# A four-layer conv and attention network on one core: attention's preparation and settling in smaller parts, and the second layer's gate laid between the first norms of the feed-forward layer

## The chip, the cores and the metric

The kernel runs on one core of a Trainium2 chip. The time is the device time of one execution in microseconds (us), the median of several runs. PE is TensorE (matmul), PEld its weight load, DVE is VectorE, ACT is ScalarE, POOL is GpSimd, SP is SyncE, which here issues DMAs. All data is float32.

## The reference, cut to what matters

X has 4 images of 128 channels and 64 x 64 places; as tokens these are 4 x 4096 rows of 128. Four layers follow each other. The change touches the end of the second, the start of the third and the attention of the fourth.

```python
# layer 1, its end: o is the scan's output, normed over the batch
g = sigmoid(einsum('bihw,io->bohw', o, conv4_w) + conv4_b)
x = g * x + x
# layer 2, per token: t is the normed token
a = t + cumprod(cos(t + theta))        # heads of 8, the first replaced by the last
x1 = layernorm(a);  q = cos(phi) * cos(x1[:8])
t = t + layernorm(x1 + relu(q @ w1.T + b1) @ w2.T + b2)
# layer 3, attention over 4096 tokens of one image
f = v @ W1[:h];  g = v @ W1[h:]        # 16 numbers per token, v the normed token
e[i, j] = exp(sum_a w2[a] * tanh(f[i, a] + g[j, a] + b1[a]) + b2)   for j < i
t[i] += sum_j e[i, j] * v[j] / (sum_j e[i, j] + 1e-10)
```

## The kernel before

X stays in SBUF, [128, 4 x 4096]. `layer1`, `layer2` and `attention` issue most of their work through `InOrder` (L69 on), which keeps every engine's queue in the order of the source. In the profile all of these instructions therefore stand under line L82, and are told apart by the names of their tiles.

**The gate, end of `layer1` (L1419 to L1444).** The scan leaves its output in DRAM, 32 blocks of 512 columns, `kept` (L1314 stores `o`). After the batch statistics (`mv`, `sc`, `sb`, L1404 to L1416) `gate(k)` loads one block (`oin`, L1422, four buffers), multiplies by `conv4_w` into `psg`, takes the sigmoid on ACT (`g`) and computes X = (g + 1) X on DVE. `to_tokens(k - 2)` turns the block before the last into tokens with four transposes (`psf`), copied back into X by DVE for odd and by ACT for even blocks. 34 steps, each with a gate and a turn, but for the two ends.

**The feed-forward layer, `layer2`.** X is now 128 tiles of 128 tokens; a group is 8 tiles (two of the gate's blocks). `slot(p, s)` (L1730) is written out by hand: p is the group, s one of eight slots. Slot s does the matmuls and rectifiers of group p, and steps of the groups around it: the first norm of group p + 3 (`moments A` in slot 0, `variance`, `root` in slot 3, `a_norm` in 4, `a_turns`, `a_less`), the cosines and products of group p + 2 (slot 0: Abs and Sin on ACT, `a_products` on POOL), its second norm (B, slots 2 to 5), and the third (D) of group p - 1. The loop starts at p = -3, so three passes come before the first matmul (`phh`, `hid`, `pff`). Its weights w1T and w2T are loaded by SP at the start (L118, L1539).

**Attention, `attention` (L1994).** For each image there are 8 query blocks of 512 tokens (`ib`, called block 0 to 7). Block ib runs over the keys in 4 ib + 3 rounds (`blocks`, L2124): 4 ib + 1 of full width, one with the parts 384 and 128 wide, one 256 wide. 544 rounds in all. The tanh is split into factors, so that a round (`products`, L2133) is: 4 row groups of matmuls of the maps F and G give the denominators in D (three banks) and the numerators `num` of the round two before; ACT takes Ln of D and Exp of the result (r, 128 x 1536, together with the finished e of an earlier round 128 x 2048); DVE multiplies r by num (128 x 1024 and 128 x 512); POOL adds the three parts. Two rounds later ACT's Exp gives e, DVE masks the diagonal (`keep`, four masks, in rounds 1 to 3 of the next block), and PE multiplies e by v (`acc`).

`side` chooses which of the two sets of banks of D a round uses; they share two banks. The fourth bank is also the one in which everything else is turned or mapped (`aux`). A round in which it is so used (`taken`), and the one behind it, stay on side 0. Where a round uses the same side as the last (`again`), its order on PE differs, since it must wait for the last Ln.

Two kinds of work are laid between the rounds. `prepare(n, q)` (L2089) makes the next block's v, F and G: for even q `statistics` (L2071, 8 bn_stats, 6 small DVE operations, Ln and Exp for rstd), v from X (4 operations, part 1), transposes and vT (part 2), four maps (parts 3 to 6: matmul, Exp on ACT, then the largest value into `top` on DVE, and for G a product on POOL), an end (7). `settle` (L2233) turns the weighted sum: `zs`, `den`, `zl`, and the additions into X, seven rounds after a block's last. These lines spread the parts:

```python
PARTS, ON_BANK = 8, (2, 3, 4, 5, 6)
to = -(-PARTS * max(r - first + 1, 0) // (rounds - first))
step((n, ib, parts, r == rounds - 1), range(done, max(done, to)))
```

Of the kernel before, what the change touches and what calls it, by code (L numbers as in the profile page):

```python
# [8 lines left out]
F32 = mybir.dt.float32  # L9
# [7 lines left out]
P = 128  # L17
NB = 4
# [70 lines left out]
class Kernel:  # L89
# [816 lines left out]

    def layer1(self):

# [4 lines left out]
        nc = plain  # L917
        NG = 8
        GS = NT // NG
        with ExitStack() as ctx:  # L920
            cp = ctx.enter_context(tc.tile_pool(name="l1c", bufs=1))
            sp = ctx.enter_context(tc.tile_pool(name="l1s", bufs=2))
            gp = ctx.enter_context(tc.tile_pool(name="l1g", bufs=2))
            kp = ctx.enter_context(tc.tile_pool(name="l1k", bufs=2))
            dram = ctx.enter_context(tc.tile_pool(name="l1d", bufs=1, space=DRAM))
            pm = ctx.enter_context(tc.tile_pool(name="l1pm", bufs=4, space=PSUM))
            pp = ctx.enter_context(tc.tile_pool(name="l1pp", bufs=1, space=PSUM))

# [2 lines left out]

            lin1_w = self.load(cp, "lin1_w", [P, P])
            fc_in4 = self.load(cp, "fc_in4", [P, P])
            conv4_w = self.load(cp, "conv4_w", [P, P])


            wx = self.load(cp, "in_w4", [P, 2, 257])
# [466 lines left out]
            mv = sp.tile([P, 2], F32, name="mv")  # L1404
            nc.vector.bn_aggr(mv, bst)
            sc = sp.tile([P, 1], F32, name="sc")
            sb = sp.tile([P, 1], F32, name="sb")
            nc.scalar.activation(sc, mv[:, 1:2], AF.Sqrt, bias=self.eps5)
            nc.vector.reciprocal(sc, sc)
            nc.vector.tensor_mul(sc, sc, self.col("bn_g"))  # L1410
# [3 lines left out]
            nc.tensor.matmul(ps[:, 0:1], conv4_w, sb, start=True, stop=True)  # L1414
            nc.vector.tensor_add(sb, ps[:, 0:1], self.col("conv4_b"))
            nc.vector.tensor_scalar(conv4_w, conv4_w, sc, None, ALU.mult)  # L1416
            nc = InOrder(tc)

            def gate(k):  # L1419
                ks = slice(k * 512, (k + 1) * 512)  # L1420
                o = gp.tile([P, 512], F32, name="oin", tag="tm", bufs=4)
                plain.sync.dma_start(o, kept[k])  # L1422
                ps = mm("psg")
                nc.tensor.matmul(ps, conv4_w, o, start=True, stop=True)
                g = gp.tile([P, 512], F32, name="g", tag="yT")
                nc.scalar.activation(g, ps, AF.Sigmoid, bias=sb)
                nc.vector.scalar_tensor_tensor(X[:, ks], g, 1.0, X[:, ks], ALU.add, ALU.mult)

            def to_tokens(k):
                ps = mm("psf")  # L1430
                for v in range(4):
                    c = k * 512 + v * P
                    nc.tensor.transpose(ps[:, v * P:(v + 1) * P], X[:, c:c + P], self.ident)
                dst = X[:, k * 512:(k + 1) * 512]
                if k % 2:
                    nc.vector.tensor_copy(dst, ps)
                else:
                    nc.scalar.copy(dst, ps)

            for k in range(NB * NG + 2):  # L1440
                if k < NB * NG:
                    gate(k)
                if k >= 2:
                    to_tokens(k - 2)  # L1444

    def flip(self):

# [65 lines left out]
    def layer2(self):  # L1513
# [8 lines left out]
        with ExitStack() as ctx:  # L1522
# [22 lines left out]
            cphi = cp.tile([P, 8], F32, name="cphi")  # L1545
            self.cos(cp, cphi, self.row("phi"), [P, 8], "cphi")

            nc = InOrder(tc)
            V, S, G = nc.vector, nc.scalar, nc.gpsimd

            def bcast(name):
# [1 line left out]

            def stream(g):
                return T[:, g * GT:(g + 1) * GT, :]

            st = {}

# [165 lines left out]
            def on(g, step, *args):  # L1724
                if 0 <= g < NG:
                    step(*([g] + list(args)))

            ON_VECTOR = ((0, 1, 3), (1,), (1,), (1, 3), (1,), (1,), (1, 3), (1,))

            def slot(p, s):  # L1730
# [47 lines left out]
                else:  # L1778
                    on(a, a_less)
                    on(b, b_turns)  # L1780

            for p in range(-3, NG + 1):
                for s in range(8):
                    slot(p, s)

# [206 lines left out]
    def attention(self):  # L1994
# [14 lines left out]
        with ExitStack() as outer:  # L2009
# [7 lines left out]
            with ExitStack() as ctx:  # L2017
# [52 lines left out]

                def statistics(t0):  # L2071

                    st = sp.tile([P, 8, 6], F32, name="st")
                    mean = sp.tile([P, 8], F32, name="mean")
                    rstd = sp.tile([P, 8], F32, name="rstd")
                    d = sp.tile([P, 8], F32, name="d")
                    for k in range(8):
                        nc.vector.bn_stats(st[:, k, :], T[:, t0 + k, :])
                    nc.vector.tensor_add(mean, st[:, :, 1], st[:, :, 4])
                    nc.vector.tensor_scalar(mean, mean, 0.5, None, ALU.mult)  # L2080
                    nc.vector.tensor_sub(d, st[:, :, 1], st[:, :, 4])
                    nc.vector.tensor_mul(d, d, d)
                    nc.vector.tensor_add(rstd, st[:, :, 2], st[:, :, 5])
                    nc.vector.scalar_tensor_tensor(rstd, d, 32.0, rstd, ALU.mult, ALU.add)
                    nc.scalar.activation(rstd, rstd, AF.Ln, bias=self.eps5, scale=1.0 / P)
                    nc.scalar.activation(rstd, rstd, AF.Exp, scale=-0.5)
                    norm[0] = mean, rstd

                def prepare(n, q):  # L2089

                    v = vs[q]
                    if q % 2 == 0:
                        statistics(n * NT + 4 * q)
                    yield
                    mean, rstd = norm[0]
                    for k in range(4):
                        t = n * NT + 4 * q + k
                        nc.vector.tensor_scalar(v[:, k, 0:LAST], T[:, t, 0:LAST], mean[:, t % 8:t % 8 + 1],
                                                rstd[:, t % 8:t % 8 + 1], ALU.subtract, ALU.mult)
                    yield  # L2100
                    pd = aux()
                    for k in range(4):
                        aside(nc.tensor.transpose(pd[:, k * P:(k + 1) * P], v[:, k, :], self.ident))
                    vT = rp.tile([P, 512], F32, name="vT", bufs=1)
                    uses[:] = [nc.vector.tensor_copy(vT, pd)]
                    wrote[0] = None
                    yield
                    out = {"v": v, "F": [], "G": []}
                    for k, (to, m) in enumerate((("F", wf[0]), ("F", wf[1]), ("G", wg[0]), ("G", wg[1]))):
                        ps = aux()  # L2110
                        aside(nc.tensor.matmul(ps, m, vT, start=True, stop=True))
                        t = bp.tile([P, 512], F32, name=f"{to}{k % 2}" + (f"_{q}" if to == "G" else ""),
                                    bufs=1 if to == "G" else 3)
                        uses[:] = [nc.scalar.activation(t, ps, AF.Exp, scale=2.0)]
                        wrote[0] = t
                        out[to].append(t)
                        yield
                        nc.vector.tensor_reduce(top[:, 8 * n + q, k:k + 1], t, AX.X, ALU.max)
                        if to == "G":
                            nc.gpsimd.tensor_scalar(t, t, cw[k % 2], None, ALU.mult)  # L2120
                    pieces[n, q] = out
                    yield
# [110 lines left out]
                def settle(n, ib, aT):  # L2233
# [4 lines left out]
                    zs = ep.tile([P, 512], F32, name="zs", bufs=1)  # L2238
                    uses[:] = [nc.vector.tensor_copy(zs, z)]
                    wrote[0] = None  # L2240
                    z = zs.rearrange("p (s c) -> p s c", c=P)
                    den = sm.tile([P, 4], F32, name="den")
                    nc.vector.tensor_scalar(den, z[:, :, LAST], tiny, None, ALU.add)
                    nc.vector.reciprocal(den, den)
                    zl = sm.tile([P, 4], F32, name="zl")
                    nc.vector.tensor_reduce(zl, z[:, :, 0:LAST], AX.X, ALU.add)
                    nc.vector.tensor_mul(zl, zl, den)
                    t0 = n * NT + 4 * ib
                    for s in range(4):
                        tt = T[:, t0 + s, 0:LAST]  # L2250
# [5 lines left out]


                order = [(n, q) for n in range(NB) for q in range(8)]
                for _ in prepare(*order[0]):
                    pass  # L2260
                later = [lambda *a: a, weigh, settle]
                LAG = 4 + len(later)
                waiting, sums = [None, None], [None, None]
                spaces = [rp.tile([P, 4, 512], F32, name="r", bufs=RB) for k in range(2)]
                held = [None] * len(later)
                PARTS, ON_BANK = 8, (2, 3, 4, 5, 6)
                last = [0, False]

                def step(block, parts=()):


                    taken = held[-1] is not None or any(p in ON_BANK for p in parts)
                    side = int(last[0] == 0 and not taken and not last[1])
                    again = side == last[0]
                    last[:] = side, taken
# [6 lines left out]
                        next(ahead)  # L2282

                for k, (n, ib) in enumerate(order):
                    ahead, done = (prepare(*order[k + 1]), 0) if k + 1 < len(order) else (None, PARTS)
                    todo = list(blocks(ib))
                    rounds = len(todo)

                    first = 4 + LAG if ib == 7 else 0
                    for r, parts in enumerate(todo):  # L2290
                        to = -(-PARTS * max(r - first + 1, 0) // (rounds - first))
                        step((n, ib, parts, r == rounds - 1), range(done, max(done, to)))
                        done = max(done, to)
                for k in range(LAG):
                    step(None)
                nc = self.nc
# [110 lines left out]
@with_exitstack  # L2407
def tile_conv_attn_hybrid(ctx: ExitStack, tc: tile.TileContext, ins: dict, out: bass.AP):
    k = Kernel(ctx, tc, ins, out)
    k.layer0()  # L2410
    k.layer1()
    k.layer2()
    k.attention_maps(ctx)
    k.moe(2)
    k.attention()
    k.moe(3)
    k.flip()
# [79 lines left out]
```

## Time and profile before

| | us |
|---|---|
| median of 3 runs (lowest, highest) | 5567.05 (5563.71, 5577.1) |
| the profiled execution: its time, its span | 5584.88, 5583.2 |
| layer 1's scan and what is before it, to the end of the statistics | 0 to 1937.8 |
| the gate | 1937.8 to 1985.8 |
| three passes of norms before the steady feed-forward layer | 1985.8 to 2050.5 |
| feed-forward layer in its steady state, last pff at | 2691 |
| attention, first and last multiplication by num | 3093.1 to 5192.5 |
| the second expert layer's last pex, the flip to the output | 5542, to 5583.2 |

PE is busy 4990.0 us (89% of the span), DVE 4020.2, ACT 3113.5, POOL 3102.9; the mean granted TensorE clock is 0.941. A row of a timeline gives start, duration, engine, source line, operation, written and read tiles, their shape and a count, and in brackets how long the engine had been idle before it and what released it. A row of the stages gives the stretch, its length and the busy time of PE, PEld, DVE, ACT and POOL, each with its number of instructions, then the clock granted to PE (1 is full), the DMA share and GB/s. A row of waits gives who waited for whom, the total in us, how often, and the longest.

### The profile page before, as it was taken

Reading aid. Unit: us, or ns where it says so; the run is one execution under the profiler, and the core shown is the slowest. Engines: PE = TensorE matmul, PEld = TensorE weight load, DVE = VectorE, ACT = ScalarE, POOL = GpSimd, SP = SyncE. Lnnn points to the kernel's source line nnn. Section 1 sums busy time; section 2 is a strip of 40 time slices with the busy share of each in tenths; the row PEclk is TensorE's granted clock in tenths of the full one; section 3 lists DMA queues with packets and bytes.
Section 4 is the critical chain, followed back from the end, with each engine's and each line's share of the span. In section 5 each row is a group of like instructions: output and inputs, shape, how many; then the busy total and the mean of one; then the engine's idle time right before and its main releaser. Section 6 shows DMA issues by size and latency. Waiting matters only on the chain. (4 is left out here: it accounts for less than half of the span.)

```text
span 5583.2 us, 62833 instructions
## 1 busy us (share of the span) xinstructions
PE 4990.0 (89%) x21718; PEld 2405.5 (43%) x21718; DVE 4020.2 (72%) x7854; ACT 3113.5 (56%) x3785; POOL 3102.9 (56%) x3027
## 2 busy tenths in 40 slices
PE   5898999879999859999887899989998998999887
PEld 3454444436666523333443344434443444444443
DVE  6888898758875577886697665666566666665796
ACT  1221222146654445555421789878988997889431
POOL 0625355414443334543498567666766776667597
PEclk8999999989988779999899899999999999999899
DMA  5545455300000110000000000000000000000001
GB/s 173 133 124 127 127 143 129 83 6 5 12 16 16 41 44 1 1 1 1 6 31 31 1 1 1 1 1 1 1 1 1 1 1 1 1 1 1 5 1 61
DMA packets 66743, 185.21 MB, mean 33 GB/s; under 512 B 13158, under 2 KB 16038, under 8 KB 64744
## 3 DMA queue, kind: packets, MB, share of 16 engines
q1 hardware_dynamic: 55792, 163.68, 9.9%
q0 software_dynamic: 6272, 12.86, 1.4%
q10 hardware_dynamic: 4344, 4.50, 0.3%
q8 instruction: 175, 2.87, 0.2%
q14 instruction: 160, 1.31, 0.1%
HBM read 131.63 MB, written 49.36 MB: 32 GB/s over the span
## 5 line engine op out<-in xcount | busy, mean ns | idle before, releaser
L82 POOL TENSOR_TENSOR r<-r 128x512 f32<-128x512 f32 (+1 forms) x1088 | 1348.7, 1241 | 666.1 <-DVE r L82 610.3
L82 DVE TENSOR_TENSOR r<-r,num 128x1024 f32<-128x1024 f32 (+1 forms) x1088 | 969.9, 926 | 565.0 <-PE num L82 518.1
L82 PE MATMUL D<-F,G 32*128 32x512 f32 (+3 forms) x4608 | 1223.1, 591 | 1.9 <-POOL G L82 1.0
L82 PE MATMUL num<-F,G 32*128 32x512 f32 (+3 forms) x4608 | 1090.1, 606 | 105.0 <-DVE r L82 101.0
L82 ACT ACTIVATE r<-r 128x2048 f32<-128x2048 f32 (+4 forms) x610 | 1018.4, 1679 | 49.2 <-POOL r L82 3.4
L82 ACT ACTIVATE r<-D 128x1536 f32<-128x1536 f32 (+1 forms) x544 | 764.2, 1405 | 210.4 <-PE D L82 178.2
L82 PE MATMUL acc<-pr,ident 128*128 128x512 f32 x1600 | 736.2, 609 | 63.2 <-DVE pr L82 63.0
L82 PEld LDWEIGHTS D<-F,G 32*128 32x128 f32 x4608 | 505.3, 190 | 326.0 <-issue 216.3
L82 PE MATMUL acc<-r,v 128*128 128x512 f32 (+3 forms) x1152 | 608.1, 615 | 2.9 <-DVE aT L82 2.9
L82 PEld LDWEIGHTS num<-F,G 32*128 32x128 f32 x4608 | 394.8, 187 | 414.0 <-DVE r L82 236.1
L1887 PE MATMUL pex<-w_expert_w,vT 128*128 128x512 f32 x1024 | 490.8, 619 | 77.6 <-DVE x L1890 77.5
L1897 POOL TENSOR_TENSOR x<-x 128x512 f32<-128x512 f32 (+2 forms) x576 | 472.3, 820 | 103.5 <-DVE x L1890 73.4
L82 POOL DMA_INDIRECT px<-tab,idx x196 | 359.4, 1834 | 295.1 <-DVE idx L82 158.5
L82 PEld LDWEIGHTS acc<-pr,ident 128*128 128x128 f32 x1600 | 303.7, 195 | 414.1 <-issue 330.3
L82 DVE TENSOR_TENSOR pr<-v,wt 128x2560 f32<-128x2560 f32 x160 | 453.9, 2843 | 30.7 <-PE acc L82 23.6
L82 PE MATMUL pff<-hid,w_ffn_w2T 128*128 128x512 f32 x1024 | 468.9, 601 | 0.0
L1890 DVE TENSOR_TENSOR x<-pex,gate 128x1024 f32<-128x1024 f32 x256 | 309.0, 1213 | 61.5 <-POOL X L1898 49.9
L82 PEld LDWEIGHTS acc<-r,v 128*128 128x128 f32 x1152 | 177.6, 191 | 395.8 <-issue 266.3
L1887 PEld LDWEIGHTS pex<-w_expert_w,vT 128*128 128x128 f32 x1024 | 184.8, 194 | 328.0 <-DVE x L1890 174.2
L82 ACT ACTIVATE hid<-phh,cols 128x512 f32<-128x512 f32 x320 | 198.9, 685 | 224.7 <-PE phh L82 224.7
L82 POOL TENSOR_TENSOR Y<-y,tm 128x64 f32<-128x64 f32 x256 | 115.4, 471 | 331.9 <-DVE w L82 159.9
L82 POOL TENSOR_TENSOR X<-X,sl 128x512 f32<-128x512 f32 x32 | 90.1, 2817 | 376.1 <-ACT sl L82 376.1
(563 smaller groups left out, 7390.4 us busy)
## 6 DMA issues: line engine op xcount, KB each, us to landing
v<-tab SPq DMA_DIRECT2D x320, 256.0 KB, 3.9
oms<-omw SPq DMA_DIRECT2D x32, 432.0 KB, 3.3
omr<-oms SPq DMA_DIRECT2D x32, 432.0 KB, 4.4
X<-in_x_dram SPq DMA_DIRECT2D x8, 1024.0 KB, 10.6
tab<-vb SPq DMA_DIRECT2D x64, 128.0 KB, 2.7
o<-o SPq DMA_DIRECT2D x32, 256.0 KB, 2.0
oin<-o SPq DMA_DIRECT2D x32, 256.0 KB, 2.8
kept<-X SPq DMA_DIRECT2D x4, 2048.0 KB, 6.3
```

What stands on the lines that cost most here:

```text
L82: return lambda *args, **kwargs: self.tc.keep_in_program_order(op(*args, **kwargs))
L1887: nc.tensor.matmul(pex[:, 4 * h:4 * h + 4, :], vT[:, k, :], ew[:, 512 * h:512 * (h + 1)], start=True, stop=True)
L1890: nc.vector.tensor_tensor(x, pex, gate[:, k, :].unsqueeze(2).to_broadcast([P, NE, P]), ALU.mult)
L1897: nc.gpsimd.tensor_tensor(x[:, 0:w, :], x[:, 0:w, :], x[:, w:2 * w, :], ALU.add)
```

## The change

The gate leaves `layer1`, which only keeps `conv4_w`, `sb` and the DRAM blocks alive (`gate_maps`). `layer2` runs four gate steps before its first pass, and then 11, 11 and 8 between the slots of the three passes. All turned blocks are now copied by ACT. `psg` and `psf` use the four banks of `phh`. The statistics of attention are cut in three parts (numbered -3 to -1, even q only), the empty first part of odd q is gone, settling is cut in three steps over three rounds (`settle`, `ratio`, `onto`), and the parts are dealt out one a round from the first round on, as soon as they fit, instead of evenly over the block.

```diff
-            nc = InOrder(tc)
-            def gate(k):
...
-            def to_tokens(k):
...
-            for k in range(NB * NG + 2):
-                if k < NB * NG:
-                    gate(k)
-                if k >= 2:
-                    to_tokens(k - 2)
+            self.gate_maps = conv4_w, sb, kept
...
+            def gate(k):
+                if k < NK_:
+                    ks = slice(k * 512, (k + 1) * 512)
+                    o = gp.tile([P, 512], F32, name="oin", bufs=4)
+                    plain.sync.dma_start(o, kept[k])
+                    ps = ph.tile([P, 512], F32, name="psg", tag="phh")
+                    nc.tensor.matmul(ps, conv4_w, o, start=True, stop=True)
+                    x = gp.tile([P, 512], F32, name="g")
+                    S.activation(x, ps, AF.Sigmoid, bias=gate_b)
+                    V.scalar_tensor_tensor(self.X[:, ks], x, 1.0, self.X[:, ks], ALU.add, ALU.mult)
+                if k >= 2:
+                    ps = ph.tile([P, 512], F32, name="psf", tag="phh")
+                    for v in range(4):
+                        c = (k - 2) * 512 + v * P
+                        nc.tensor.transpose(ps[:, v * P:(v + 1) * P], self.X[:, c:c + P], self.ident)
+                    S.copy(self.X[:, (k - 2) * 512:(k - 1) * 512], ps)
...
+            GATES, LAST_GATES = (0, 1, 1, 1, 2, 2, 2, 2), (0, 1, 1, 1, 2, 2, 1, 0)
...
+            steps = iter(range(NK_ + 2))
+            for _ in range(4):
+                gate(next(steps))
             for p in range(-3, NG + 1):
                 for s in range(8):
                     slot(p, s)
+                    for _ in range(GATES[s] if p < -1 else LAST_GATES[s] if p < 0 else 0):
+                        gate(next(steps))
...
                 def statistics(t0):
                     st = sp.tile([P, 8, 6], F32, name="st")
+                    for h in range(2):
+                        for k in range(4 * h, 4 * h + 4):
+                            nc.vector.bn_stats(st[:, k, :], T[:, t0 + k, :])
+                        yield
...
-                    for k in range(8):
-                        nc.vector.bn_stats(st[:, k, :], T[:, t0 + k, :])
...
                     norm[0] = mean, rstd
+                    yield
...
                     if q % 2 == 0:
-                        statistics(n * NT + 4 * q)
-                    yield
+                        yield from statistics(n * NT + 4 * q)
...
                     wrote[0] = None
-                    z = zs.rearrange("p (s c) -> p s c", c=P)
+                    return n, ib, zs.rearrange("p (s c) -> p s c", c=P)
+
+                def ratio(n, ib, z):
                     den = sm.tile([P, 4], F32, name="den")
...
                     nc.vector.tensor_mul(zl, zl, den)
+                    return n, ib, z, den, zl
+
+                def onto(n, ib, z, den, zl):
...
-                later = [lambda *a: a, weigh, settle]
+                later = [lambda *a: a, weigh, settle, ratio, onto]
...
-                PARTS, ON_BANK = 8, (2, 3, 4, 5, 6)
+                PARTS = 7
...
-                    taken = held[-1] is not None or any(p in ON_BANK for p in parts)
+                    taken = held[SETTLES] is not None or any(1 <= p <= 5 for p in parts)
...
-                        to = -(-PARTS * max(r - first + 1, 0) // (rounds - first))
-                        step((n, ib, parts, r == rounds - 1), range(done, max(done, to)))
-                        done = max(done, to)
+                        now = ()
+                        if ahead is not None and r >= first:
+                            now = range(done, done - (done - PARTS) // (rounds - r))
+                            done = now.stop
+                        step((n, ib, parts, r == rounds - 1), now)
```

`done` starts at 0 for odd q and at -3 for even q of the block that is prepared, and at round `first` = 13 (11 before) in block 7.

More of the change, by code (lines that the diff above doesn't have):

```diff
@@ L905, in layer0_gather, with layer1 @@
                         nc.vector.tensor_add(xs, xs, sl)
-    def layer1(self):
+    def layer1(self, after):
         tc, X = self.tc, self.X
@@ L919, in layer1 @@
         GS = NT // NG
+        dram = after.enter_context(tc.tile_pool(name="l1d", bufs=1, space=DRAM))
+        ga = after.enter_context(tc.tile_pool(name="l1a", bufs=1))
         with ExitStack() as ctx:
@@ L924, in layer1 @@
             kp = ctx.enter_context(tc.tile_pool(name="l1k", bufs=2))
-            dram = ctx.enter_context(tc.tile_pool(name="l1d", bufs=1, space=DRAM))
             pm = ctx.enter_context(tc.tile_pool(name="l1pm", bufs=4, space=PSUM))
@@ L933, in layer1 @@
             fc_in4 = self.load(cp, "fc_in4", [P, P])
-            conv4_w = self.load(cp, "conv4_w", [P, P])
+            conv4_w = self.load(ga, "conv4_w", [P, P])
             wx = self.load(cp, "in_w4", [P, 2, 257])
@@ L1406, in layer1 @@
             sc = sp.tile([P, 1], F32, name="sc")
-            sb = sp.tile([P, 1], F32, name="sb")
+            sb = ga.tile([P, 1], F32, name="sb")
             nc.scalar.activation(sc, mv[:, 1:2], AF.Sqrt, bias=self.eps5)
@@ L1416, in layer1 @@
             nc.vector.tensor_scalar(conv4_w, conv4_w, sc, None, ALU.mult)
-            nc = InOrder(tc)
-            def gate(k):
[L1420 to L1427, printed above, removed]
-            def to_tokens(k):
[L1430 to L1438, printed above, removed]
-            for k in range(NB * NG + 2):
-                if k < NB * NG:
-                    gate(k)
-                if k >= 2:
-                    to_tokens(k - 2)
+            self.gate_maps = conv4_w, sb, kept
     def flip(self):
@@ L1546, in layer2 @@
             self.cos(cp, cphi, self.row("phi"), [P, 8], "cphi")
-            nc = InOrder(tc)
+            plain, nc = nc, InOrder(tc)
             V, S, G = nc.vector, nc.scalar, nc.gpsimd
@@ L1555, in stream @@
                 return T[:, g * GT:(g + 1) * GT, :]
+            conv4_w, gate_b, kept = self.gate_maps
+            gp = ctx.enter_context(tc.tile_pool(name="l2g", bufs=2))
+            NK_ = len(kept)
+            def gate(k):
[14 more added lines that the diff above has]
+                    S.copy(self.X[:, (k - 2) * 512:(k - 1) * 512], ps)
             st = {}
@@ L2258, in attention @@
                 order = [(n, q) for n in range(NB) for q in range(8)]
+                PARTS = 7
                 for _ in prepare(*order[0]):
                     pass
-                later = [lambda *a: a, weigh, settle]
+                later = [lambda *a: a, weigh, settle, ratio, onto]
+                SETTLES = 2
                 LAG = 4 + len(later)
@@ L2284, in attention @@
                 for k, (n, ib) in enumerate(order):
-                    ahead, done = (prepare(*order[k + 1]), 0) if k + 1 < len(order) else (None, PARTS)
+                    ahead = done = None
+                    if k + 1 < len(order):
+                        ahead, done = prepare(*order[k + 1]), 0 if order[k + 1][1] % 2 else -3
                     todo = list(blocks(ib))
@@ L2410, in tile_conv_attn_hybrid @@
     k.layer0()
-    k.layer1()
-    k.layer2()
+    with ExitStack() as gate:
+        k.layer1(gate)
+        k.layer2()
     k.attention_maps(ctx)
```

## The prediction

> **What bounds the kernel now.** First the page's busy line, then the busy time by stage, then rows of the two places that the change touches.
>
> ```profile
> PE 4990.0 (89%) x21718; PEld 2405.5 (43%) x21718; DVE 4020.2 (72%) x7854; ACT 3113.5 (56%) x3785; POOL 3102.9 (56%) x3027
> ```
> ```profile
> 1937.80:1985.80 48.00, 45.09 (x192) 25.79 (x192) 33.92 (x56) 32.62 (x53) 2.35 (x3) 0.94 0.59 176
> 1985.80:2050.50 64.70, 9.52 (x26) 3.82 (x27) 47.13 (x139) 16.51 (x22) 27.75 (x25) 0.52 0.00 1
> ...
> 3200.00:5100.00 1900.00, 1772.61 (x9788) 774.90 (x9786) 1192.11 (x1833) 1645.93 (x1178) 1303.05 (x1039) 0.98 0.00 1
> ```
>
> The stage rows give start and end, length, then busy PE, PEld, DVE, ACT, POOL, the granted clock, the DMA share and GB/s. The gate (first row) is 48.0 us with PE full: 45.1 of 48. The feed-forward layer's first three norms (second row) are 64.7 us in which PE has 9.5 us of work at half clock; DVE, ACT and POOL hand one group of eight tokens' tiles to each other. Little is shared between the two, so laying one into the other can pay. Attention (third row) has PE at 93%, ACT at 87%, DVE at 63%: its cost is in stalls. Those show on ACT, DVE and PE around one settling, near 3869:
>
> ```profile
> 3865.69 1.45 ACT L82 ACTIVATE r<-D 128x1536 f32<-128x1536 f32 x1
> 3867.24 1.91 ACT L82 ACTIVATE r<-r 128x2048 f32<-128x2048 f32 x1
> 3869.29 1.45 ACT L82 ACTIVATE r<-D 128x1536 f32<-128x1536 f32 x1
> 3870.83 1.91 ACT L82 ACTIVATE r<-r 128x2048 f32<-128x2048 f32 x1
> 3875.85 1.45 ACT L82 ACTIVATE r<-D 128x1536 f32<-128x1536 f32 x1 [3.11 <-PE D L82]
> ```
> ```profile
> 3867.18 0.69 DVE L82 COPY zs<-D 128x512 f32<-128x512 f32 x1 [0.86 <-ACT r L82]
> ...
> 3869.08 1.13 DVE L82 SCALAR_TENSOR_TENSOR X<-zs,den,X 128x127 f32<-128x127 f32 x4
> 3870.13 0.16 DVE L82 TENSOR_TENSOR X<-X,zl 128x4 f32<-128x4 f32 x1
> 3870.20 1.81 DVE L82 TENSOR_TENSOR r<-r,num 128x1024 f32<-128x1024 f32 x2
> ```
> ```profile
> 3868.59 0.59 PE L82 MATMUL D<-F,G 32*128 32x512 f32 x1
> 3869.11 1.12 PE L82 MATMUL acc<-r,v 128*128 128x512 f32 x2
> 3872.07 1.23 PE L82 MATMUL num<-F,G 32*128 32x512 f32 x3 [1.84 <-DVE r L82]
> 3873.08 1.07 PE L82 MATMUL num<-F,G 32*128 32x512 f32 x3
> ```
>
> A round starts with the Ln of D. Most rounds start 3.34 us apart, which is Ln and Exp back to back: ACT sets the pace. DVE's two multiplications by num take 1.82 us of it and leave 1.36 us idle ("3838.78 1.82", idle 1.36 before). Settling puts zs, den, zl and X into one round: 3867.18 to 3870.29, 3.1 us. So the next multiplication comes late, PE waits 1.84 us for it, runs at half clock afterwards (1.07 us where it was 0.59), and the next Ln is 6.56 us after the last.
>
> The waits of the stage, summed:
>
> ```profile
> PE num L82 <- DVE r L82: 101.0, 96, 2.9
> ACT rstd L82 <- DVE rstd L82: 20.4, 12, 3.9
> ```
>
> Over 544 rounds the Ln starts span about 2097 us. With 3.34 us for each full round, 2.22 for each of the 32 that are half as wide, 0.48 for each of the 120-odd map Exps and 0.5 for each statistic the stage would be 1850. So some 247 us are stalls; nothing else in attention can be won.
>
> **A rule against the row.** The Trainium skill (TensorE: Matmul & The Clock Gate, Part 1) holds that the clock is halved after an idle window of about 3.4 us. By that the 1.84 us gap costs 1.84. The rows show 1.0 to 1.2 us matmuls after it, and 1.08 after a gap of 1.16 at 3854.8; the period grew by 3.2. I take the row: by it the 24 settlings counted below are worth 40 us, by the rule (1.84 of each 3.2) about 23.
>
> **The change, part by part: attention.**
> Settling in three. zs (0.69) stays in its round; den and zl (3867.91 to 3869.08, 1.17) go to the next, the additions into X (1.12) to the one after. Each is under the 1.36 us idle; where a map is made in the same round the reduction of 0.68 joins (1.85), but that round is 3.82 long and its idle 1.84. In image 1 the period behind the settling was 5.4, 5.1, 5.0, 6.6, 5.4 and 5.2 for query blocks 2 to 7, so 1.6, 1.5, 1.6, 3.2, 2.0 and 1.8 too long, 1.95 in the mean. I leave 0.3 for waits on the transposes: 1.65 x 24 = 40 us. From below: nothing, if the late DVE only shifts; from above 47.
> Statistics in three. Eight bn_stats and the six small operations (2.93 us, 3840.52 to 3843.45) become two rounds of 0.82 and one of 1.26 with Ln and Exp behind it. For query blocks 3 and 5 the last now lies in round 2, where DVE also waits for Exp before two masks. The first five rounds of block 5 took 22.5 us before against 16.7 unhindered; by hand I get 21.5. Gain about 1.0 x 8 = 8; from below -10 (ACT waiting 1.3 us behind the masks in eight places), from above 20.
> The norm (v, 1.1 to 1.7 us) moves from rounds 1 to 3 of blocks 2, 4 and 6 into round 0, ahead of the masks: block 4 had 6.5 behind it where the same round of block 7, which has no part there, had 4.2. I take 1.3 a block, 12 blocks: 15; ends 0 and 25.
> Packing. Parts follow each other from the first round on instead of being spread. By the code's rule rounds that use the same set as the last fall from 241 to 180; such a round without a map takes 3.58 (median) against 3.35. Gain 61 x 0.23 = 14 at most; I take 10, for maps themselves keep their 0.48.
> Blocks 0 and 1, 3 and 7 rounds: ten parts in seven rounds now where eight were; block 0 has two maps in its second round instead of three (8.9 to 11.7 us in that round). Statistic, norm, masks and transposes meet in block 1. Some 2 us an image: 8; ends -15 and 20.
> Sum: 40 + 8 + 15 + 10 + 8 = 81, and I take 80. Two more closing rounds (LAG 9 for 7) hold only the split settling that the last settling did before: nothing.
>
> **The change: the gate.** PE keeps its 192 matmuls, DVE its 32 multiplications (22.1 us); 16 copies go from DVE (0.68) to ACT (0.58, +9.2 us). Each step then needs 1.30 of ACT, 1.30 of PE. In ACT's order the tables go from nine loads to fourteen between the scan's end and the first gated feed-forward group: five more.
>
> ```profile
> 1996.77 1.06 ACT L82 ACTIVATE a<-a 128x1024 f32<-128x1024 f32 x1 [8.69 <-DVE a L82]
> 1997.85 1.28 ACT L82 ACT_TABLE_LOAD   x1
> 1999.14 1.15 ACT L82 ACTIVATE a<-a,halfpi 128x1024 f32<-128x1024 f32 x1
> ```
>
> The skill (ScalarE: Activation LUTs, What ACT_TABLE_LOAD costs) puts 2.66 us on a switch, drain included: 13.3 for five. Here the load starts 0.02 after one activation and the next starts 0.01 after it: 1.28, so 6.4 us, and I take that.
> The loads of oin move on SP's queue behind w2T (5.0 us to land), the last store and four loads of w1T (3.0 us of issue); the four early ones that now lie in the scan are gone. First gate matmul near 1940.8, 3 us later than now.
> Worked by hand in queue order from there: the first four steps end at 1949 (11 us after 1937.8). The pass for group 0, that is from one moments A to the next, is 12.2 us now and takes eleven gates: 11 x 1.26 + 2.6 of loads + waits on PE after a cold gap, 21.8. The second was 27.2 and becomes 32: DVE holds the multiplications behind moments B, which wait for POOL's products (6.6 us from Sin), and ACT's root holds the next sigmoid. The third was 28.5 and becomes 33. So 48 goes, 11 + 9.6 + 4.8 + 4.5 + some 2 for half clock come: gain 16. From below -6: each of the 34 steps at half clock is 2.6 us on PE, 88 in all, and with the 30 us of waits that PE stands in, longer than the 112.7 of now. From above 40: DVE's own 22.1 + 47.1 us with 3 of lateness. The middle is nearest to the walk, so 16.
>
> **The sum.** 80 + 16 = 96. The profiled execution took 5584.9 (span 5583.2 and 1.7 around it), 17.8 above the median of the runs shown, 5567.05; I subtract from both alike: 5488.9 profiled, 5471 for the median.
>
> **Rivals.**
> Slower: packing meets the masks. Rounds 1 to 4 of each of 28 blocks hold four masks that wait for Exp, and one stall of about 3.5 us. If vT, reductions and small operations bring DVE over its 1.36 us in a second of these rounds, each block has one more gap over 1.2 us and its half clock: 3.4 x 28 = 95, against 80 of which then only settling's 40 and the gate's 16 stay: +39, 5606. It decides from more than about 17 such blocks on. For it: in block 1 one round took 10.7. Against: consecutive map rounds of block 2 ran at 3.8 to 3.9, which is ACT's own sum.
> Nothing from attention: the lag of DVE is handed on to the masks' stall and no Ln starts earlier; only the gate's 16 stay: 5551. Against it speaks that the rounds behind a settling return to 3.34 at once, so the loss there is final.
> Half: settling pays, the packed parts give it back partly: 40 + 16 - 15 = 41, 5526.
> More: masks and parts merge into one stall and DVE is never late by over 1 us: 120 + 25 = 145, 5422. For it: each PE gap avoided also avoids its half clock.
>
> **How the numbers follow.** Forecast (5435 to 5501) 0.55; half (5501 to 5550) 0.23; more 0.10; only the gate 0.06; slower 0.06. 0.3% is 17 us and about what a measurement of this kernel can tell from no change: faster 0.88, same 0.06, slower 0.06. Leaving out the ends beyond 137 and under 27 us of gain gives 5430 to 5540.
>
> **What would show it.** Rounds behind a settling at 3.4 to 3.9 and zs, den and X in three rounds; PE's wait for DVE r in num at 50 to 70 us instead of 101; rstd's wait under 20; fewer half-clock stretches (granted clock over 0.98). For the gate: first hidden rows near 2034 instead of 2050, 14 table loads, PE's clock under 0.8 in the stage. It is wrong if block 3 and 5 grow in their first five rounds, or if the second and third pass take over 40 us.

## The result and the profile after

| | before | after |
|---|---|---|
| median of 11 runs each, us | 5568.56 (5558.8 to 5596.71) | 5550.27 (5534.45 to 5555.81) |
| after / before | | 0.9953 (95%: 0.9938 to 0.9968) |
| profiled execution, span, us | 5583.2 | 5542.0 |
| first Ln of attention to last | 2110.7 | 2091.0 |
| bn_aggr (the end of layer 1's batch statistics) to the first hidden row that DVE makes | 111.7 | 99.5 |
| first pslin (layer 1's first matmul of the scan) to bn_aggr, not changed | 795.8 | 786.3 |

By the ratio the kernel is 26 us faster (by the medians 18); 96 were forecast. The two profiles differ by 41: 9.5 of it lie in layer 1's scan, in which all kernels of this study do the same work, and which took between 778 and 806 us in eleven profiled executions. Stages are therefore compared below, not spans: attention came out equal within 1.3 us where it was the same code as before, and within 5.1 where it was the same as after; the gate's stage within 2.6. Counted to the first Ln of attention, the gate's gain is as large as in the table: 1143.4 us behind bn_aggr before, 1130.4 after.

The busy line of after, then its rows by stage (the gate among the norms; attention), columns as before:

```profile
PE 4985.9 (90%) x21718; PEld 2394.6 (43%) x21718; DVE 4071.4 (73%) x7838; ACT 3122.8 (56%) x3806; POOL 3109.6 (56%) x3027
```
```profile
1932.90:2026.50 93.60, 62.56 (x216) 32.89 (x217) 68.21 (x168) 59.77 (x90) 33.17 (x25) 0.83 0.29 84
3053.00:5144.00 2091.00, 1961.06 (x10821) 848.01 (x10818) 1379.14 (x2035) 1812.45 (x1301) 1437.35 (x1145) 0.97 0.00 1
```

DVE does fewer instructions than before and is busy 51 us longer. That is the first sign: some of its instructions became slower. X's additions alone took 703 ns each in the mean, where 343 was usual before. One settling of after, on ACT, DVE and GpSimd (POOL), in query block 4 of image 1:

```profile
3768.64 1.43 ACT L82 ACTIVATE r<-D 128x1536 f32<-128x1536 f32 x1
3770.16 1.91 ACT L82 ACTIVATE r<-r 128x2048 f32<-128x2048 f32 x1
3771.98 1.43 ACT L82 ACTIVATE r<-D 128x1536 f32<-128x1536 f32 x1
3773.51 1.91 ACT L82 ACTIVATE r<-r 128x2048 f32<-128x2048 f32 x1
3776.40 1.45 ACT L82 ACTIVATE r<-D 128x1536 f32<-128x1536 f32 x1 [0.98 <-PE D L82]
```
```profile
3767.80 1.80 DVE L82 TENSOR_TENSOR r<-r,num 128x1024 f32<-128x1024 f32 x2
3769.53 2.94 DVE L82 SCALAR_TENSOR_TENSOR X<-zs,den,X 128x127 f32<-128x127 f32 x4
3772.39 0.16 DVE L82 TENSOR_TENSOR X<-X,zl 128x4 f32<-128x4 f32 x1
3772.46 1.81 DVE L82 TENSOR_TENSOR r<-r,num 128x1024 f32<-128x1024 f32 x2
```
```profile
3766.57 5.22 POOL L82 TENSOR_TENSOR r<-r 128x512 f32<-128x512 f32 x4
3773.75 2.62 POOL L82 TENSOR_TENSOR r<-r 128x512 f32<-128x512 f32 x2 [1.96 <-DVE r L82]
```

The round with zs (3761.70) and the one with den and zl (3765.28) last 3.58 and 3.36 us, as forecast. But the four additions into X, 1.13 us before, take 2.94; the multiplication behind them comes late and the round from 3771.98 is 4.42 long. POOL adds r from 3766.57 to 3771.79. Before, the same four additions stood from 3869.08 to 3870.21, and POOL was idle from 3868.16 on:

```profile
3865.54 2.62 POOL L82 TENSOR_TENSOR r<-r 128x512 f32<-128x512 f32 x2 [0.93 <-ACT r L82]
3871.56 2.61 POOL L82 TENSOR_TENSOR r<-r 128x512 f32<-128x512 f32 x2 [3.40 <-DVE r L82]
```

### The profile page after: what moved, and what is told of

It is laid out like the page before. It is cut to its first block, busy times and chain, and to the rows that moved or that the text cites. A ratio compares the mean times of both kernels' runs of the same rounds, so it can differ in the third digit from the quotient of the medians.

```text
span 5542.0 us, 62850 instructions
## 1 busy us (share of the span) xinstructions
PE 4985.9 (90%) x21718; PEld 2394.6 (43%) x21718; DVE 4071.4 (73%) x7838; ACT 3122.8 (56%) x3806; POOL 3109.6 (56%) x3027
## 5 line engine op out<-in xcount | busy, mean ns | idle before, releaser
L82 PE MATMUL D<-F,G 32*128 32x512 f32 (+3 forms) x4608 | 1237.3, 587 | 1.0 <-POOL G L82 1.0
L82 PE MATMUL num<-F,G 32*128 32x512 f32 (+3 forms) x4608 | 1079.1, 601 | 79.7 <-DVE r L82 78.3
## 6 DMA issues: line engine op xcount, KB each, us to landing
X<-in_x_dram SPq DMA_DIRECT2D x8, 1024.0 KB, 10.7
```

Source lines behind the costliest of these rows:

```text
L82: return lambda *args, **kwargs: self.tc.keep_in_program_order(op(*args, **kwargs))
```

## The experiments

All on the same measure: the whole time against before in the same series, and attention from first to last Ln of the profiled execution (before 2110.7, after 2091.0).

| run | whole, ratio (95%) | attention, us |
|---|---|---|
| e1 gate only | 0.9959 (0.9943 to 0.9976) | 2109.4 |
| e2 attention only | 0.9964 (0.9948 to 0.9979) | 2096.1 |
| e3 settling in three only | 0.9983 (0.9974 to 0.9991) | 2099.4 |
| e4 after, X in four rounds | 0.9869 (0.9847 to 0.989) | 2049.5 |
| e5 after, POOL quiet beside X | 0.986 (0.9838 to 0.9882) | 2047.5 |
| e6 after, parts placed | 0.9908 (0.9885 to 0.9931) | 2071.7 |
| e7 settling in six only | 0.9937 (0.992 to 0.9955) | 2076.9 |
| e8 preparation ahead | 0.9822 (0.98 to 0.9843) | 2004.8 |
| e9 e8 with oin first | 0.9819 (0.9797 to 0.9841) | 2006.7 |

**Taking the change apart.** e1 joins the new layers 1 and 2 with the old attention, e2 the reverse.

> The kernel before with only the gate moved between the first norms (attention as before). The forecast's working says 16 us less than before; the trace of after shows 12 us less from the scan's end to the first gated feed-forward group (104.6 against 116.8), and a scan that ended 9.5 us earlier after the first pslin. Theory A (the gate's place is all of it): 12 us less, and the stage from the first pslin to bn_aggr within 3 us of before. Theory B (the four early loads of oin, which stood in SP's queue during the scan and are gone, also held the scan's stores): 20 to 22 us less, with that stage 8 to 10 us shorter again. Rival (only the attention moved the time): within 4 us of before.

> The kernel before with only the attention changed (gate as before). The forecast's working says 80 us less than before. From the trace of after (first to last Ln of attention 2091.0 against 2110.7, and 2.4 us given back behind it) I now expect 17 us less, with query blocks 0 and 1 longer by 5 and 13 us over the four images and blocks 2, 4 and 6 shorter by 10 to 12 each. Rival (the gate alone made the gain and attention's part of the trace is one execution's chance): within 5 us of before.

e1: bn_aggr to the first hidden row 99.5 us, as in after; the scan took 795.2, as in before. Over all profiles the scan took 778 to 806 us in the seven runs without the early loads of oin and 782 to 796 in the four with them. So these loads did not hold the scan; theory B falls, and the 9.5 us of the profiles are scatter. By the whole time e1 is 23 us faster (13 to 32), more than the 12 to 13 of its stage; where the rest comes from stays open. e2: 14.6 us off attention; blocks 0 and 1 longer by 8.0 and 11.8, blocks 2, 4 and 6 shorter by 10 to 11, as expected.

e3 takes before and splits only the settling:

```diff
-                    z = zs.rearrange("p (s c) -> p s c", c=P)
+                    return n, ib, zs.rearrange("p (s c) -> p s c", c=P)
+                def ratio(n, ib, z):
...
+                def onto(n, ib, z, den, zl):
...
-                later = [lambda *a: a, weigh, settle]
+                later = [lambda *a: a, weigh, settle, ratio, onto]
```

> The kernel before with only the settling in three rounds (zs; den and zl; X); preparation's parts, their places and the gate as before. The forecast counted 40 us for this (24 settlings, 1.65 us each). Theory A (the X additions now stand behind the multiplication by num, where GpSimd adds, take 2.9 us instead of 1.1, and so a settling still costs about 1.0 of the 1.95 us): 15 to 25 us less than before, X additions at 2.5 us or more for four and a round of 4.4 behind them. Theory B (the packed parts took back what settling gave): 35 to 45 us less, rounds behind a settling at 3.4 to 3.9. Theory C (a late DVE is only handed on): within 5 us of before.

11.3 us, a little under theory A's 15; theory B's 35 is excluded. X took 692 ns each (343 before). The round behind zs fell (5.2 to 3.4 in block 7), and one of 4.4 appeared behind X.

**What slows X.** e4 spreads the additions, e5 quiets POOL:

```diff
-                later = [lambda *a: a, weigh, settle, ratio, onto]
+                later = [lambda *a: a, weigh, settle, ratio] + [lambda *a, s=s: onto(s, *a) for s in range(4)]
```
```diff
+                        if held_onto[0]:
+                            nc.gpsimd.memset(q[:, cs0], 1.0)
+                        else:
                             nc.gpsimd.tensor_tensor(q[:, cs0], r0[:, k2, cs0], r0[:, k2 + 1, cs0], ALU.add)
                             nc.gpsimd.tensor_tensor(q[:, cs0], q[:, cs0], r0[:, k1, cs0], ALU.add)
```

> The changed kernel, with the four additions of a settling into X in four rounds, one each, instead of in one (a second buffer for zs; three more closing rounds). Theory A (four additions beside GpSimd's own are more than the 1.36 us that DVE has idle in a round, one is 0.7 and fits): the round behind X goes from 4.4 to 3.4 in blocks 2, 4, 6, 7 and from 5.1 to about 3.9 in 3 and 5, 28 settlings by 1.0: some 25 us less than the changed kernel, 5525 where that is 5550. Theory B (DVE's lateness is not what makes that round long): within 4 us of the changed kernel.

> The changed kernel, but in the rounds in which a settling is added into X, GpSimd's two additions of r are left out and a memset stands in their place, so those rounds weigh with ones: part of the computation is left out, for the time alone. Theory A (the additions into X read two SBUF operands and stand still while GpSimd's additions run): four additions at 1.1 to 1.3 us instead of 2.9, the round behind X at 3.4 instead of 4.4 in blocks 2, 4, 6 and 7, and 3.4 to 3.9 instead of 5.1 in 3 and 5; first to last Ln 35 to 45 us shorter than after's 2091, like the kernel with the additions in four rounds (2049). Theory B (the four additions are slow because of their own place behind the multiplications, whatever GpSimd does): still 2.5 us or more, and first to last Ln within 8 us of 2091.

e5, same settling, DVE and POOL:

```profile
3771.90 1.80 DVE L82 TENSOR_TENSOR r<-r,num 128x1024 f32<-128x1024 f32 x2
3773.63 1.12 DVE L82 SCALAR_TENSOR_TENSOR X<-zs,den,X 128x127 f32<-128x127 f32 x4
3774.68 0.15 DVE L82 TENSOR_TENSOR X<-X,zl 128x4 f32<-128x4 f32 x1
3775.02 1.82 DVE L82 TENSOR_TENSOR r<-r,num 128x1024 f32<-128x1024 f32 x2 [0.19 <-PE num L82]
```
```profile
3770.67 2.64 POOL L82 TENSOR_TENSOR r<-r 128x512 f32<-128x512 f32 x2
3773.26 0.52 POOL L82 MEMSET r<- 128x512 f32 x1
3776.32 2.63 POOL L82 TENSOR_TENSOR r<-r 128x512 f32<-128x512 f32 x2 [2.54 <-DVE r L82]
```

With POOL's additions gone the four take 1.12 us again, in the same place in DVE's order, and the rounds behind X are 3.3 to 3.4 in blocks 2 to 7; attention loses 43.5 us. Theory B of e5 falls. e4 leaves POOL as it was:

```profile
3771.45 1.05 DVE L82 SCALAR_TENSOR_TENSOR X<-zs,den,X 128x127 f32<-128x127 f32 x1
3772.84 1.82 DVE L82 TENSOR_TENSOR r<-r,num 128x1024 f32<-128x1024 f32 x2 [0.34 <-PE num L82]
3774.58 0.98 DVE L82 SCALAR_TENSOR_TENSOR X<-zs,den,X 128x127 f32<-128x127 f32 x1
3775.98 1.82 DVE L82 TENSOR_TENSOR r<-r,num 128x1024 f32<-128x1024 f32 x2 [0.41 <-PE num L82]
```
```profile
3774.14 2.63 POOL L82 TENSOR_TENSOR r<-r 128x512 f32<-128x512 f32 x2 [0.43 <-DVE r L82]
```

One addition still takes about 1 us where it needs 0.3: it ends at 3775.56, just behind the first of POOL's two (1.3 us from 3774.14). But one such wait fits into DVE's 1.36 us of idle time, the line keeps 0.34 to 0.42 of it, and four in a row did not. 41.5 us, more than the 25 expected; the same as e5, so spreading buys back all of it.

All of after's trace agrees: of X's 128 additions the 74 with no POOL instruction beside them took 0.34 to 0.35 us, the 54 with one 0.45 to 1.44. The 128 x 1024 multiplication by num took 1.20 to 1.22 with POOL beside it (383 times) and without (129).

The Trainium skill (SBUF — State Buffer, SBUF: two separate sides) has the rule: VectorE and GpSimd share a pair of ports, which one instruction takes whole, and whichever starts first blocks the other. On VectorE's side this holds for an operation in a 2-port mode, and for one with two SBUF inputs, the latter against a GpSimd operation that reads SBUF. The rows fit the second kind: r<-r,num, which reads num from PSUM, took 1.80 to 1.82 us with POOL busy or not; X, with zs and X in SBUF, ended behind POOL's additions, and without these did not wait. That the ports are the cause is the skill's word; that POOL's additions are is shown.

**How much the settling is worth.** e7 is e3 with the additions in four rounds.

> The kernel before with only the settling changed: zs, den and zl, then the four additions in four rounds; parts, their places and the gate as before. The forecast's term for settling was 40 us. Theory A (the term was right but for GpSimd holding the additions): first to last Ln 35 to 45 us shorter than before's 2110.7, where the settling in three rounds gave 11. Theory B (the packed parts of the changed kernel are needed for it, the spread ones fill the rounds behind the settling): 25 us at most. Whole time 5535 to 5545 by A where before is 5580.

33.8 us off attention with the old parts where they were, against 11.3 in e3: close to theory A's 35, and over B's 25.

**The parts' places.** e6 is after with these rounds:

```diff
+                LATE = ((-3,), (-2,), (), (), (), (-1,), (), (0,), (1,), (2,), (3,), (4,), (5,), (6,))
+                PLACED = {1: ((-3, -2), (-1, 0), (1,), (2,), (3,), (4,), (5, 6)), 3: LATE, 5: LATE}
```

> The changed kernel with only the places of the parts changed in query blocks 1, 3 and 5: in 3 and 5 the statistic's end waits for round 5, behind the masks, and no part stands in the settling's round 6; in block 1 transposes and first map are in rounds of their own. Theory A (parts that meet masks or a settling are what made 3 and 5 no shorter and 1 longer): blocks 3 and 5 at about 40.2 instead of 43.6 us over ten rounds, 24 to 28 us over their eight occurrences; block 1 some 5 us an image, 20; first to last Ln at 2040 to 2055 instead of 2091. Theory B (what the parts cost is handed on wherever they are): within 8 us of 2091.

19.3 us, half of what I expected: 14.0 in blocks 3 and 5, 5.6 in block 1. Of block 5's round 2 the statistic's end is gone, but a half of bn_stats still stands there between a mask and the multiplications, and it took 5.97 us (6.49 in after); and vT now stood behind X, held by POOL (2.85), in a round of 5.62.

e8 puts e4 and e6 together and prepares an image's second block in the last block of the image before; e9 puts the first four oin loads ahead of the weights' in layer 2's code.

> The changed kernel with the additions into X in four rounds, the parts of blocks 1, 3 and 5 placed as in the run with places, and the preparation of an image's second block made in the last block of the image before (the first image's ahead of the loop), so that block 0 holds only two of a statistic's parts. By theory A of the runs before, what they give adds up: 42 for the additions, 25 for blocks 3 and 5, 20 for block 1, and block 0 at 11 to 13 us an image instead of 21, some 30 in three images and a part of it in the first: first to last Ln at about 1975 to 1990, the whole at 5425 to 5445 where the changed kernel is 5553. If lateness is only moved about, not less than 2035.

> The kernel with preparation ahead, and the gate's first four loads of oin issued on SP ahead of the loads of w1T and w2T. In after the first gate matmul starts 10.1 us behind bn_aggr (before: 4.1), of which PE stands 6.4 for oin behind 3.0 us of SP's w1T issues and w2T's transfer. Theory A (the gate falls short of its forecast by that late start): first gate matmul 4 to 7 us behind bn_aggr, and bn_aggr to the first hidden row 94 to 97 us instead of 99.6. Theory B (the passes are bound by ACT and DVE and swallow an earlier start): 99 to 100 us as before. Whole time within 6 us of the kernel with preparation ahead, 5478.

e8: 86 us less than after between the first Ln and the last, 37 of it in block 0 and 18 in block 1. But 14.4 of it only moved: with the first image's second block prepared ahead of the loop, the first Ln comes 1144.8 us behind bn_aggr, in after 1130.4. So 72 are gained, as the whole time says: by the ratios 99 us less than before, after 26. The median is 5477.9 against 5580.5 of before. That beats both kernels; even with the moved part, attention is short of the 1975 to 1990 expected.

e9 says little of the gate. Its first gate matmul is 10.4 us behind bn_aggr, not earlier than after's 10.1: SP waited 2.6 us for the last store o<-o, and in SP's queue w2T and three of the four w1T loads still went first, whatever the order in the code. 97.4 us to the first hidden row is no evidence, since e5 and e6, with after's layers 1 and 2, had 97.2 and 97.3. The granted clock separates the two groups. Behind bn_aggr it was half from 2.4 to 2.6 us on until 16.0 to 16.2 in the four runs of 99.5 to 99.8 us, and from 2.9 to 3.1 until 13.2 to 13.3 in the three of 97.2 to 97.4, whose first pass starts 1.2 to 1.7 us sooner. Stage rows of after and of e5, from 13.2 and 13.4 us behind bn_aggr on:

```profile
1936.00:1938.70 2.70, 2.70 (x6) 1.13 (x5) 1.07 (x2) 1.01 (x2) 0.00 (x0) 0.50 0.66 178
1956.20:1959.00 2.80, 2.80 (x14) 1.71 (x13) 1.58 (x3) 2.25 (x4) 0.00 (x0) 1.00 0.66 213
```

What sets how long the clock stays half there stays open.

## Why the forecast had the direction and not the size

The terms, with what the runs gave (block sums over four images, single executions, each good to about 5 us; the stages as above):

| term | forecast | measured | the same where X is in four rounds |
|---|---|---|---|
| settling | 40 | 11 (e3 against before) | 34 (e7 against before) |
| norm and packing (packing forecast over all blocks), measured in blocks 2, 4, 6 | 25 | 32 (after against e3) | 34 (e4 against e7) |
| statistics, blocks 3 and 5 | 8 | -11 (same) | 2 (same) |
| blocks 0 and 1 | 8 | -15 (same) | -16 (same) |
| block 7 | 0 | 2 (same) | 8 (same) |
| attention | 80 | 20 | 61 |
| gate | 16 | 13 (six profiles against four) | |

So POOL's hold on X took some 42 of the 60 us that attention fell short: about 23 in the settling's term, 13 in the statistics', 6 in block 7. Of what is left, blocks 0 and 1 are the largest part, 24 short of their term; settling and statistics are 6 short each, and the other terms gave more than forecast.

**Settling: the step that failed.** "Each is under the 1.36 us idle" took X at 1.12 us from a row in which POOL was idle, and so put POOL's hold at nothing. In before, the burst zs, den, zl, X ran so late that POOL had finished. Split, X stands right behind the multiplications that start POOL. It took 2.94, and the new stall replaced half to all of the old one. Without that, the term is 34 of 40, so the count (24 settlings by 1.65) was about right.

The half clock, by which the forecast chose 40 over 23, was not the reason. In before, it follows only 4 of the 24 settlings, block 5's in each image, where PE had stood for 1.84 us; the row at 3869 is one of these. Around the other 20 PE stood for 0.8 to 1.2 us at a time, and the period still grew, at full clock, to between 4.8 and 5.4. Block 7 of image 1, PE and the stage row, then the stage row of block 5:

```profile
4054.05 0.70 PE L82 MATMUL num<-F,G 32*128 32x512 f32 x3 [1.16 <-DVE r L82]
4054.61 0.59 PE L82 MATMUL D<-F,G 32*128 32x512 f32 x1
4047.00:4059.00 12.00, 10.84 (x58) 4.42 (x58) 8.49 (x17) 9.81 (x7) 7.48 (x7) 1.00 0.00 1
3872.10:3875.40 3.30, 3.30 (x16) 1.19 (x16) 1.12 (x1) 0.64 (x1) 1.99 (x2) 0.50 0.01 2
```

So a gap of 1.16 us was followed by half clock at 3854.8 and by full clock here: its length alone does not decide. (Before's Ln starts span 2110.7 us, not the forecast's 2097.)

The wait for DVE's multiplication, after:

```profile
PE num L82 <- DVE r L82: 78.3, 98, 1.8
ACT rstd L82 <- DVE rstd L82: 26.5, 12, 2.6
```

78.3 us, not the 50 to 70 forecast; in e4 it is 60.0. The wait for rstd, 26.5, is not under 20 either, and attention's granted clock is 0.97, not over 0.98.

**Statistics.** By hand the first five rounds of block 5 came to 21.5; they took 21.7, with ACT standing for rstd, as feared, some 1.06 us of it for mean, which stood beside POOL (1.23 instead of 0.17):

```profile
3813.58 1.91 ACT L82 ACTIVATE r<-r 128x2048 f32<-128x2048 f32 x1
3818.10 0.30 ACT L82 ACTIVATE rstd<-rstd,eps 128x8 f32<-128x8 f32 x1 [2.61 <-DVE rstd L82]
```

The loss lies behind, in rounds that the sum did not look at: rounds 5 to 9 took 22.0 us, in e3 18.5 (some 1.0 of the difference are maps that moved there). The packed parts arrive with the settling. X, held by POOL, and a reduction make a round of 5.1; and where zs and a map share the round PE's map waits for zs before num can start, 5.4:

```profile
3831.42 0.60 PE L82 MATMUL D<-ident,aT 128*128 128x128 f32 x4
3833.10 1.13 PE L82 MATMUL D<-vT,wf 128*128 128x512 f32 x2 [1.08 <-DVE zs L82]
3834.16 0.70 PE L82 MATMUL num<-F,G 32*128 32x512 f32 x3
```

With X spread (e4 against e7) the term is 2 instead of -11; parts moved off the masks and zs, with the hold still there (e6), gave 14.

**Blocks 0 and 1.** The forecast gained 8 from fewer maps in a round; after lost 15, near its lower end (-15). In block 1 vT now stands behind two masks and aT, and the first map comes in that round:

```profile
4130.55 0.66 DVE L82 TENSOR_TENSOR r<-r,keep 128x128 f32<-128x128 f32 x2 [0.50 <-ACT r L82]
4131.13 0.68 DVE L82 COPY aT<-acc 128x512 f32<-128x512 f32 x1
4131.73 0.68 DVE L82 COPY vT<-D 128x512 f32<-128x512 f32 x1
```
```profile
4132.46 2.07 PE L82 MATMUL D<-vT,wf 128*128 128x512 f32 x2 [3.76 <-DVE vT L82]
4134.47 1.23 PE L82 MATMUL num<-F,G 32*128 32x512 f32 x3
```

PE stands 3.76 us and then runs at half speed (2.07 for two where 1.12 is usual; granted clock 0.50 from 4131 to 4136): that round is 10.6 to 10.7 us long in every image, 3.8 to 4.5 in before (where the next round was the long one, 4.1 to 10.7). It is the slower rival's mechanism, in four blocks of 28, not in 17. It is not all of the loss: in e6, with the parts in other rounds, the same round took 6.6 to 6.9 us, but block 1's last round then took 5.0 to 8.4 (3.0 to 5.0 in after), and only 5.6 us came back. The rest of these blocks' loss stays open.

**Norm and packing** gave more than forecast: in block 4 of image 1 the longest round falls from 6.81 us (e3) to 4.64, and from its eighth round on every full one but that behind X takes 3.34 to 3.36.

**The gate** was right in kind (fourteen table loads, as counted; the stage's clock was 0.83, where under 0.8 was forecast): 98.8 us (mean of six) instead of 111.6 (mean of four). The passes took 19.5, 34.7 and 33.9 us, against 21.8, 32 and 33 forecast. (Before's first hidden rows stand at 2039.1 on ACT and 2045.4 on DVE, not at the forecast's 2050.) The first gate matmul came 6.0 us later than before, not 3, with PE idle for oin:

```profile
1932.88 5.46 PE L82 MATMUL psg<-oin,w_conv_w 128*128 128x512 f32 x6 [6.37 <-DMA oin<-o]
```

**The rivals.** 5550 is the number of "only the gate", by accident: attention gave 15 to 20 us too, which that rival denied. "Half" had the right shape, settling that pays and parts that partly give it back, but not POOL, which took more than the parts did. Neither the slower case nor the one with more came.

## What to carry to other kernels

A duration read from a trace holds for what the other engines did at that moment: before moving a DVE operation on SBUF tiles, look at what GpSimd does at its new place, and take its duration from a row where GpSimd is as busy. Where it must lie beside GpSimd, one operation per round can hide where four in a row can't. And a part packed forward needs its new round looked at for what it queues behind (masks, copies), not only for its own length.

## What was not expected of the hardware

In the gate's stage the same shows at larger size; DVE, then POOL:

```profile
1985.02 0.69 DVE L82 TENSOR_SCALAR k<-c 128x1024 f32<-128x1024 f32 x1
1985.74 2.37 DVE L82 TENSOR_SCALAR k<-k 128x1024 f32<-128x1024 f32 x1
1988.03 3.09 DVE L82 SCALAR_TENSOR_TENSOR X<-g,X 128x512 f32<-128x512 f32 x2
```
```profile
1983.98 5.99 POOL L82 TENSOR_TENSOR x<-x,rows 128x1024 f32<-128x1024 f32 x2 [1.96 <-DVE x L82]
```

k, with one SBUF input, waited too: 2.37 instead of 0.69 us. So did den in attention: 0.54 us at 3766.10, beside POOL, and 0.23 in the one case of after without. So two SBUF inputs are not needed. The skill's rule also names 2-port modes. k's 0.69 us for 1024 columns, where a<-k,c with two SBUF inputs takes 1.21 alone, would fit such a mode; no run here shows which mode it ran in. The first k took 0.69 beside POOL's first instruction. That one lasted 3.58 us and the second 2.33, so there it may be POOL that waited; this was not tried.
